# Moving the tests of a bound check to the last group but one, and a copy behind four exponentials

## The chip, the core and the metric

The kernel runs on one core of a Trainium2 chip. The metric is the device time of one launch, in microseconds (us). The core has five engines that each work through their own list of instructions in order and wait for each other through semaphores: TensorE (PE, matrix products; its weight loads are shown as PEld), VectorE (DVE), ScalarE (ACT), GpSimd (POOL) and SyncE (SP), whose list holds the DMA transfers.

## The reference

Two graph layers over 64 graphs of 256 nodes with 512 features share one adjacency matrix. Layer 0 is attention with one additive score per pair of nodes, layer 1 is attention with 8 heads of 64. All is float32.

```python
# --- layer 0 (adj_preln) ---
h = jnp.maximum(_layernorm(x, axis=-1), 0.0)
x = x + _L0_gnn_ref(h, adj, L0_gnn_W, L0_gnn_a)
# --- layer 1 (adj_preln) ---
h = jnp.maximum(_layernorm(x, axis=-1), 0.0)
x = x + _L1_gnn_ref(h, adj, L1_gnn_Wq, L1_gnn_bq, ..., L1_gnn_bo)
return x
```

Layer 1 computes `q`, `k` and `v` from `h`, `scores = q k^T / 8`, masks them by the adjacency matrix, takes the softmax over the keys, weighs `v` with it and multiplies by `Wo`. The kernel leaves out the subtraction of the row maximum in the softmax. That is allowed only where the scores are bounded, so the kernel also works out a bound from the norms of the weights. If the bound fails, a second, general version of the computation (`any_inputs`) runs after the first. The bound holds for these inputs.

## The kernel before

The 64 graphs are handled as 32 groups (`g`) of two batches (`b`). A batch's 256 nodes lie on 128 partitions in two tiles. Each group goes through three stages in a pipeline over the groups: `first_norm` and `first_layer` (the two layer norms and layer 0) two groups ahead, `project` (the products for `q`, `k`, `v`) one group ahead, and `scores`, `mask_pairs`, `weigh` and `outputs` for the group itself. The strings in `steps` say in which order pieces of these stages are issued within a batch: `S` scores, `m` mask a pair of heads, `u` a projection product, `n` a norm piece, `s` a piece of layer 0, `o` an output product. A product of two 2x2-blocked matrices is done with seven block products instead of eight, so each projection consists of seven products `pq` (or `pk`, `pv`) of four matmuls each, with sums of operands made beforehand on POOL (`sums`, from `operand_sums`).

All engine calls pass through the class `Remembers` (line 35 records them). `not_sooner` and `after` add order constraints on one engine. A scheduler then orders each engine's list within these constraints and the data's own. So an edit at one place can move an instruction of another engine.

What the change touches:

- `judge` (lines 283 to 396) is the bound check. It runs as a generator, `verdict`, in pieces among the prologue's work. Its sums of squares end in a `[128, 10]` tile `norm`. Its last piece makes five tests from `norm` in 13 small DVE instructions, which write `test`, `side`, `held` and at last `wrong`, a single integer. `run(verdict)` at line 925, before the loop over the groups, finishes whatever of it is left.
- Line 51 loads `wrong` into a register on every engine, to branch on it at the end. On SP the scheduler had put that load in the prologue, between two transfers. On the other engines it stands at the end.
- The transposition of normed rows goes by way of DRAM: DVE transposes blocks of 32 x 32 into `xt`, SP writes `xt` to DRAM (`passed`), then reads it back in four parts in another order (`moved`, line 466), and ACT copies `moved` into `hT` (`put`, line 473). `put_last` remembers the last of these copies.
- `scores` (line 749) makes eight heads' scores in four pairs, into PSUM banks `sc` that come from a ring of five (`mm`), and empties each with an exponential on ACT. The exponential's order relative to `put_last` is set at line 769, for the first group's first batch alone. At that time the last `put` is that of the second group's layer 1 (`hT1`), whose two batches are copied with two instructions each.

```python
for other in [last, *put_last] if g == b == 0 and i else [last]:
    after(made, other)
```

So the exponentials of the pairs after the first (`i` from 1) come behind the second batch's copies. The projection of the second group starts right after these scores on PE: its first two products need only the first batch's copies, and its third one needs `sums`, which POOL makes from both batches' copies, and the earlier product's bank to have been copied out by ACT (`kept_q`).

Of the kernel before, what the change touches and what calls it, by code (L numbers as in the profile page):

```python
# [57 lines left out]
def bounded(  # L58
# [35 lines left out]
    NG = B // GB  # L94
# [14 lines left out]
    def mm(name):  # L109
        return psum.tile([P, 512], F32, tag="turn", name=name, bufs=5)  # L110
# [4 lines left out]
    def after(instruction, name):  # L115

        tc.add_manual_dep(
            instruction.ins, name,
            mybir.DependencyInfo(mybir.DependencyClass.NoSync, mybir.DependencyReason.DATA),
            reason="the engine's order",  # L120
        )

    def not_sooner(engine, operation, *args, **kwargs):

        last = engine.last
        after(getattr(engine, operation)(*args, **kwargs), last)
# [9 lines left out]
    def matmul(*args, **kwargs):  # L136
        in_order(nc.tensor.matmul(*args, **kwargs))  # L137
# [116 lines left out]
    def weight_sums(name):  # L254
        w = w_sb[name]
        not_sooner(vector, "tensor_sub", w[:, :, T3, :], w[:, :, W22, :], w[:, :, W12, :])
        vector.tensor_sub(w[:, :, T1, :], w[:, :, W12, :], w[:, :, W11, :])
        vector.tensor_sub(w[:, :, T2, :], w[:, :, W22, :], w[:, :, T1, :])
        vector.tensor_sub(w[:, :, T4, :], w[:, :, W21, :], w[:, :, T2, :])
# [23 lines left out]
    def judge():  # L283
# [73 lines left out]
        norm = const.tile([P, 10], F32, name="norm")  # L357
# [3 lines left out]
        gpsimd.memset(power[:, 7:8], 1.0)  # L361
        gpsimd.memset(power[:, 8:10], 1.0 / 32)
        gpsimd.tensor_tensor(norm, norm, power, op=ALU.pow)
        for _ in range(6):
            yield
        root = float(D) ** 0.5

        test = const.tile([P, 5], F32, name="test")
# [24 lines left out]
        held = const.tile([P, 1], F32, name="held")  # L393
        vector.tensor_reduce(held, test, axis=AX.X, op=ALU.min)
        vector.tensor_scalar(wrong, held[0:1, :], -1.0, 1.0, op0=ALU.mult, op1=ALU.add)
        yield

# [9 lines left out]
    put_last, sums_last = [], []  # L409
# [334 lines left out]
    def value_differences(g, b):  # L744

        v = qkv["v", g, b][0]
        not_sooner(gpsimd, "tensor_sub", v[:, 1, :], v[:, 1, :], v[:, 0, :])

    def scores(g, b):

        (q, q_tag), (k, k_tag) = (qkv[name, g, b] for name in "qk")
        name = f"{g}_{b}"
        p = att.tile([P, NQ * QH, NT, N], F32, tag="p", name=f"p_{name}", bufs=1)
        for i in range(HP):
            sc = [mm(f"sc_{name}_{2 * i + j}").rearrange("p (k n) -> p k n", k=NT) for j in range(2)]
            for kb in range(NT):
                for j in range(2):
                    rows = slice(j * DH, (j + 1) * DH)  # L760
                    matmul(
                        sc[j][:, kb, :], k[rows, i, kb * P : (kb + 1) * P], q[rows, i, :],
                        start=True, stop=True,
                    )
            pair = p[:, 2 * i : 2 * i + 2]
            for j in range(2):
                last = scalar.last
                made = scalar.activation(pair[:, j], sc[j], AF.Exp, scale=scale)
                for other in [last, *put_last] if g == b == 0 and i else [last]:
                    after(made, other)  # L770
        places.extend((q_tag, k_tag))
        return p
# [16 lines left out]
    def weigh(g, b, p):  # L789


        v, v_tag = qkv["v", g, b]
        name = f"{g}_{b}"
        total = mm(f"total_{name}").rearrange("p (q n) -> p q n", q=NQ)
        r = att.tile([P, NQ, N], F32, tag="r", name=f"r_{name}", bufs=1)
        for quad in range(NQ):
            for j in range(QH):
                matmul(
                    total[j * S : (j + 1) * S, quad, :], ones, p[:, quad * QH + j, 0, :],
                    start=True, stop=True,  # L800
                )
        for quad in range(NQ):
            not_sooner(vector, "reciprocal", r[:, quad, :], total[:, quad, :])
        for quad in range(NQ):
            pr = mm(f"pr_{name}_{quad}").rearrange("p (h n) -> p h n", h=2)
            for half in range(2):
                for kb in range(NT):
                    for j in range(QH):
                        head = quad * QH + j
                        c0 = head * DH + half * S  # L810
                        matmul(
                            pr[j * S : (j + 1) * S, half, :], v[:, kb, c0 : c0 + S],
                            p[:, head, kb, :], start=(kb == 0), stop=(kb == NT - 1),
                        )
            oT = big.tile([P, 2, N], F32, tag=f"oT{quad}", name=f"oT_{name}_{quad}", bufs=1)
            vector.tensor_mul(oT, pr, r[:, quad, None, :].to_broadcast([P, 2, N]))
            oTs[quad] = oT
        places.append(v_tag)
        quads = [oTs[c][:, :, r * P : (r + 1) * P] for r in range(2) for c in range(2)]
        sums = big.tile([P, 3, 2, P], F32, tag="o_sums", name=f"o_sums_{g}_{b}", bufs=1)  # L820
        operand_sums(vector, quads, sums)
        operands["o", g, b] = seven(quads, sums)

    def outputs(g, b):
        xt, ops = xs[g, b], operands.pop(("o", g, b))

        def product(out, i, start):
            a, w = ops[i]
            for c in range(2):
                matmul(  # L830
                    out, a[:, c, :], w_sb["o"][:, c, w, :],
                    start=start and c == 0, stop=(c == 1), skip_group_check=True,
                )

        def add(t, half, out):
            to = xt[:, t, half * D // 2 : (half + 1) * D // 2]
            vector.tensor_add(to, out, to)

        first = held_bank(2, f"py1_{g}_{b}")[:, : D // 2]
        product(first, 1, True)  # L840
        add(0, 0, first)
        yield
        second = mm(f"py2_{g}_{b}")[:, : D // 2]
        product(second, 2, True)
        add(0, 0, second)
        yield
        product(first, 6, False)
        add(1, 0, first)
        yield
        second = mm(f"py7_{g}_{b}")[:, : D // 2]  # L850
        product(second, 7, True)
        add(1, 1, second)
        yield
        product(first, 5, False)
        add(1, 1, first)
        yield
        product(second, 4, False)
        add(1, 0, second)
        if g == NG - 1:

            nc.sync.dma_start(og[g, b][:, 1], xt[:, 1])
            nc.sync.dma_start(og[g, b][:, 0, : D // 2], xt[:, 0, : D // 2])
        yield
        product(first, 3, False)
        add(0, 1, first)
        if g == NG - 1:
            nc.sync.dma_start(og[g, b][:, 0, D // 2 :], xt[:, 0, D // 2 :])
        else:
            nc.sync.dma_start(og[g, b], xt)
        yield  # L870


    def run(part):
        for _ in part:
            pass
# [54 lines left out]
    for g in range(NG):  # L930
        products = project(g + 1) if g + 1 < NG else iter(())
        pieces = first_layer(g + 2) if g + 2 < NG else iter(())
        for b, parts in enumerate(steps):
            if g == b == 0:

                parts = "Smmnnuuuumnnmussnussuunununsu"
            if waiting is not None:
                weigh(*waiting)
                late = outputs(*waiting[:2])
            for i, part in enumerate(parts):  # L940
                if part == "u":
                    next(products, None)
                elif part == "o":
                    next(late, None)
                elif part == "s":
                    next(pieces, None)
                elif part == "n":
                    next(norms, None)
                elif part == "m":
                    next(masks)  # L950
                else:
                    waiting = (g, b, scores(g, b))
                    masks = mask_pairs(waiting[2])
                if i == (len(parts) * 3 // 4, 6)[b]:
                    value_differences(g, b)
                if i == len(parts) // 2:
                    if g == b == 0:
                        weight_sums("o")
                    if b == 0 and g + 1 < NG:
                        residual(g + 1)  # L960
                    if g + 3 < NG:
                        load(g + 3, b)
        run(products)
        run(pieces)
# [373 lines left out]
```

## Time and profile before

The median of three runs is 2489.0 us.

| What | us |
|---|---|
| runs | 2487.59, 2489.0, 2489.72 |
| the profiled execution, device time | 2488.04 |
| its span, first to last instruction | 2486.4 |
| mean granted clock of TensorE | 0.998 of full |
| DVE busy in 90 to 95 us | 4.66 of 5 |
| PE busy in 95 to 100 us | 0.69 of 5 |
| PE busy in 2404.7 to 2438 us (group 30, second batch) | 33.30 of 33.30 |
| DVE busy there | 16.69 of 33.30 |

The profile is that of one execution. A busy engine is one with an instruction in work, and what an engine waited for is inferred from semaphores. The chain of waits follows the work back from the last instruction: at each step to what released it, or to the instruction before it on its engine. Times in the views count from the span's start, while a run's time includes some 1.6 us around the span.

### The profile page before, as it was taken

To read this page: it belongs to the slowest core of one execution; us is meant where nothing else is said; L and a number is where in the kernel's file an instruction comes from. 1 tells how busy PE (TensorE), PEld (TensorE's weight loads), DVE (VectorE), ACT (ScalarE), POOL (GpSimd) and SP (SyncE) were. 2 spreads that over 40 slices of the span, in tenths; PEclk is the share of its full clock that TensorE was granted. 3 is DMA by queue.
4 is the path that set the end of the run, shared out by engine and by line. 5 is a ranking of instruction groups with operands and counts; after the bars stand their busy time and mean duration, and the time that the engine had idled before them with its cause. 6 is when DMAs were issued, how large, how long until landed. Compare 5 with 4: busy or idle time off the path is not lost.

```text
span 2486.4 us, 41322 instructions
## 1 busy us (share of the span) xinstructions
PE 2456.1 (99%) x16034; PEld 2039.9 (82%) x16034; DVE 1687.1 (68%) x3002; ACT 1011.4 (41%) x2019; POOL 1017.3 (41%) x978
## 2 busy tenths in 40 slices
PE   8899999999999999999999999999999999999998
PEld 7778888888888888888888888888888888888886
DVE  6676766776666767667766667676677666676656
ACT  5443443443443434443434434344434344344321
POOL 3533444334444334444344443344443344533332
PEclk9999999999999999999999999999999999999999
DMA  6222232322232322222222323222222223232100
GB/s 191 73 90 77 68 98 81 102 80 89 75 106 77 107 79 73 91 88 95 87 84 73 107 78 105 79 80 85 92 92 95 76 75 105 81 102 79 58 26 36
DMA packets 135129, 213.58 MB, mean 86 GB/s; under 512 B 15504, under 2 KB 80272, under 8 KB 134928
## 3 DMA queue, kind: packets, MB, share of 16 engines
q1 hardware_dynamic: 134928, 210.89, 26.0%
q8 instruction: 128, 2.10, 0.3%
q14 instruction: 73, 0.60, 0.1%
HBM read 112.20 MB, written 98.63 MB: 85 GB/s over the span
## 4 chain that ended last, share of the span: by engine, by line
PE 97%; DVE 1%; DMA 0%; ACT 0%; issue 0%; SPq 0%; ACTq 0%; DVEq 0%
PE pq L137 16%; PE pk L137 16%; PE pv L137 15%; PE py L137 15%; PE sc L137 10%; PE ph L137 9%; PE pr L137 9%; PE po L137 4%; PE total L137 3%; DVE p L35 0%; DMA w_sb<-in_L_gnn_W_dram 0%; DVE r L35 0%; PE gram_q L137 0%; PE gram_k L137 0%; DVE prod L35 0%
## 5 line engine op out<-in xcount | busy, mean ns | idle before, releaser
L35 POOL TENSOR_TENSOR p<-p 128x512 f32<-128x512 f32 x256 | 409.0, 1612 | 711.5 <-DVE p L35 711.5
L35 ACT ACTIVATE p<-sc 128x512 f32<-128x512 f32 x512 | 258.0, 627 | 237.9 <-PE sc L137 233.9
L35 DVE TENSOR_TENSOR p<-p,maskT 128x1024 f32<-128x1024 f32 x256 | 340.2, 1349 | 3.9 <-ACT p L35 3.9
L35 DVE TENSOR_TENSOR x<-py,x 128x256 f32<-128x256 f32 x448 | 185.8, 415 | 169.9 <-PE py L137 160.7
L35 ACT ACTIVATE xn<-x,factor 128x512 f32<-128x512 f32 x256 | 194.5, 807 | 209.7 <-POOL factor L35 209.7
L35 DVE RECIPROCAL r<-total 128x256 f32<-128x256 f32 x128 | 215.6, 1726 | 90.1 <-PE total L137 90.1
L137 PE MATMUL py<-wo_sb,oT 128*128 128x256 f32 x1024 | 262.5, 379 | 1.7 <-DVE x L35 1.1
L137 PE MATMUL sc<-q,k 64*128 64x256 f32 x2048 | 253.5, 389 | 8.3 <-ACT p L35 8.3
L137 PEld LDWEIGHTS sc<-q,k 64*128 64x128 f32 x2048 | 211.7, 187 | 50.3 <-issue 26.3
L137 PE MATMUL pk<-hT,wk_sb 128*128 128x256 f32 x1024 | 244.7, 382 | 0.0
L137 PE MATMUL pq<-hT,wq_sb 128*128 128x256 f32 x1024 | 242.6, 385 | 0.0
L137 PE MATMUL pv<-wv_sb,hT 128*128 128x256 f32 x1024 | 236.9, 379 | 0.0
L35 POOL TENSOR_TENSOR factor<-factor,rexp 128x2 f32<-128x2 f32 x128 | 90.5, 707 | 355.2 <-DVE factor L35 355.1
L137 PE MATMUL ph<-w_sb,hT 128*128 128x258 f32 x1024 | 234.9, 381 | 0.4 <-ACT hT L35 0.3
L137 PE MATMUL pr<-p,v 128*32 128x256 f32 x4096 | 232.7, 379 | 0.0
L137 PEld LDWEIGHTS pq<-hT,wq_sb 128*128 128x128 f32 x1024 | 193.7, 192 | 36.3 <-issue 9.9
L137 PEld LDWEIGHTS pk<-hT,wk_sb 128*128 128x128 f32 x1024 | 192.1, 190 | 35.3 <-issue 10.4
L137 PEld LDWEIGHTS ph<-w_sb,hT 128*128 128x128 f32 x1024 | 194.1, 190 | 30.4 <-ACT hT L35 0.9
L137 PEld LDWEIGHTS py<-wo_sb,oT 128*128 128x128 f32 x1024 | 194.1, 190 | 29.7 <-DVE x L35 1.5
L137 PEld LDWEIGHTS pv<-wv_sb,hT 128*128 128x128 f32 x1024 | 194.5, 190 | 26.4
L137 PEld LDWEIGHTS pr<-p,v 128*32 128x32 f32 x4096 | 133.1, 110 | 87.9
L137 PE MATMUL py<-wo_sb,o_sums 128*128 128x256 f32 x768 | 197.5, 379 | 3.6 <-DVE x L35 3.6
(124 smaller groups left out, 3640.7 us busy)
## 6 DMA issues: line engine op xcount, KB each, us to landing
passed<-xt SPq DMA_DIRECT2D x124, 512.0 KB, 2.6
moved<-passed SPq DMA_DIRECT2D x496, 128.0 KB, 3.1
x<-in_x_dram SPq DMA_DIRECT2D x64, 512.0 KB, 4.4
out_dram<-x SPq DMA_DIRECT2D x62, 512.0 KB, 3.1
own<-line SPq DMA_DIRECT2D x31, 256.0 KB, 3.1
wq_sb<-in_L_gnn_Wq_dram SPq DMA_DIRECT2D x2, 512.0 KB, 9.7
wk_sb<-in_L_gnn_Wk_dram SPq DMA_DIRECT2D x2, 512.0 KB, 10.7
wv_sb<-in_L_gnn_Wv_dram SPq DMA_DIRECT2D x2, 512.0 KB, 7.5
```

The lines of the kernel that those rows point to most:

```text
L35: instruction = getattr(self.engine, operation)(*args, **kwargs)
L137: in_order(nc.tensor.matmul(*args, **kwargs))
```

## The change

The tests leave `judge` and become a function `conclude`, which is called in the second batch of the last group but one, in the middle of its pieces. `judge` ends with `norm`. The condition on the exponentials changes from `i` to `i > 1`: the second pair's exponentials no longer have to come behind the second batch's copies.

```diff
         gpsimd.tensor_tensor(norm, norm, power, op=ALU.pow)
-        for _ in range(6):
-            yield
+        norms_found.append(norm)
+        yield
+
+    norms_found = []
+
+    def conclude():
+        (norm,) = norms_found
         root = float(D) ** 0.5
 
         test = const.tile([P, 5], F32, name="test")
@@
         held = const.tile([P, 1], F32, name="held")
         vector.tensor_reduce(held, test, axis=AX.X, op=ALU.min)
         vector.tensor_scalar(wrong, held[0:1, :], -1.0, 1.0, op0=ALU.mult, op1=ALU.add)
-        yield
@@
-                for other in [last, *put_last] if g == b == 0 and i else [last]:
+                for other in [last, *put_last] if g == b == 0 and i > 1 else [last]:
                     after(made, other)
@@
                     if g == b == 0:
                         weight_sums("o")
+                    if g == max(NG - 2, 0) and b == 1:
+                        conclude()
                     if b == 0 and g + 1 < NG:
                         residual(g + 1)
```

## The prediction

> **What bounds the kernel now.** I read the page first, for the engine that sets the end, and then the chain of work.
>
> ```profile
> PE 2456.1 (99%) x16034; PEld 2039.9 (82%) x16034; DVE 1687.1 (68%) x3002; ACT 1011.4 (41%) x2019; POOL 1017.3 (41%) x978
> PE 97%; DVE 1%; DMA 0%; ACT 0%; issue 0%; SPq 0%; ACTq 0%; DVEq 0%
> ```
>
> TensorE (PE) is busy for 2456.1 of 2486.4 us and carries 97% of the chain, and the change leaves its instruction list alone. Only an idle stretch of PE can be won or lost, some 30 us in all. So I asked for PE's waits by window (us in total, times, longest).
>
> ```profile
> PE pt L140 <- ACT xn L35: 10.2, 1, 10.2
> ...
> PE sc L137 <- ACT p L35: 6.3, 2, 5.9
> ...
> PE sc L137 <- ACT p L35: 2.0, 1, 2.0
> ```
>
> The first is the first load at the start, out of reach. The second is a gap of 0.4 and one stall of 5.9 us, in 95.69 to 101.62, in the first group's first batch. The third lies at 173.85, in the second group, where no engine's order changes. The chain in order of time (start, duration, what) crosses the 5.9 us stall like this:
>
> ```profile
> 90.03 0.69 DVE v L35
> 90.72 0.79 DVE test L35
> ...
> 94.12 0.15 DVE wrong L35
> ...
> 94.28 0.48 SPq L51
> ...
> 96.53 3.35 DMA moved<-passed
> ...
> 99.94 1.14 ACT hT L35 x2
> 101.08 0.51 ACT p L35
> ...
> 101.62 2.07 PE sc L137 x6
> 103.70 9.87 PE pq L137 x40
> 113.57 3.49 PE ph L137 x16
> ```
>
> Read backwards: PE's last score matmuls wait for a PSUM bank that the third exponential (ACT p) empties; that exponential stands on ScalarE (ACT) behind the copy `hT<-moved` of the second group's second batch (call it B); that copy waits for the `moved` transfers; those stand on SP's queue behind the load of `wrong` (L51); and that waits for the last of the bound check's tests on VectorE (DVE). SP's own waits in 80 to 110 us say what it costs:
>
> ```profile
> SPq L51 <- DVE wrong L35: 7.1, 1, 7.1
> ```
>
> The clock comes last (us, PE busy, granted clock, DMA share, GB/s):
>
> ```profile
> 98.00:99.00 1.00, 0.00 (x0) 0.97 1.04 298
> 99.00:100.00 1.00, 0.00 (x0) 0.50 0.76 306
> ...
> 104.00:105.00 1.00, 1.00 (x3) 0.50 0.71 184
> 105.00:106.00 1.00, 1.00 (x4) 0.61 0.07 19
> ```
>
> The idle stretch also halves PE's clock from 98.9 to about 105.6, so about 4 us of matmuls run at half speed: 2.0 us more.
>
> [...] B's `moved` issues at 95.21, right after the register load of 94.28, though its source was in memory when the DMA traffic ended at 90.0. [...] The trace agrees for 5.9 and for 2.0 us of idle (at 173.85, clock 0.50 in 178 to 180), but 1.74 us at 2444.2 left it at 1.00. [...] `test<-norm` took 856 ns and `side<-norm` 1132 ns while POOL's residual adds ran to 92.70; the other tests took 141 to 171 ns.
>
> **The change part by part.** The order listing of both kernels shows three differences: DVE's 13 tests move from behind the last `v` add to behind the last mask multiply of group 30's second batch; the load of `wrong` on SP moves from ahead of B's `moved` to among the last output stores; B's two copies on ACT stand behind four exponentials instead of two. Besides, SP now puts the fourth `moved` of the third group's first batch (C4) behind the `passed` of its second batch (D).
>
> *Removed tests.* 13 DVE instructions in 90.64 to 94.26, 3.6 us: the third group's statistics and transposes come that much earlier, and `passed` of its first batch goes from 97.37 to about 93.8. Nothing on PE waits for these directly.
>
> *Removed SP wait.* `passed` of B issued at 86.82 and its traffic was over by 90.0 (91.0 if it took the 4.2 us of the next `passed`, 97.37 to 101.59). B's four `moved` can then issue at 90.0 instead of 95.21, and land 4.66 us later as before (95.21 to 99.87): 94.7, at worst 95.7.
>
> *ACT's order.* Up to the second exponential nothing changes: it ends at 94.94. A queued exponential takes 2.54/5 = 0.51. Then: two more exponentials to 95.95, in which time B has landed even at its worst; B's copies, 1.04 to the next start, 97.0; four exponentials 2.03, 99.0; two `xn` 1.51, 100.5; `kept_q` 0.84, 101.4. PE: the third exponential ends at 95.45, so the last scores follow at once (seventh score's first half ended at 95.69), to 96.5; two products `pq` at 1.73 each, 99.95. The third product accumulates into the bank that `kept_q` reads, so it waits for 101.4: a new stall of 1.4 us, in place of 5.9. GpSimd's two `sums` for it take 1.26 and at most 2.13 from 97.0: 100.4, not later. In the profile the third product starts three products before `ph`: 113.57 - 3 x 1.73 = 108.38. So 108.38 - 101.4 = 7.0 us are won, the 2.0 of half clock included, provided 1.4 us of idle doesn't halve the clock. I take that it doesn't, since 1.74 us didn't[...]. A gain from it is excluded, since an idle PE does no work.
>
> *C4.* D's `passed` needs the two `xn` (100.5) and a DVE transpose of 0.7: 101.3. C4 follows at 101.65 and lands in 3.0 (the median) to 4.1: 104.7 to 105.7. Its copy on ACT comes behind the third `kept_q`, that is 101.4 + 2 x 1.73 + about 1 = 105.9. Cost nothing, hidden by those three products; without that cover it is microsecond for microsecond in front of `ph`, then some 1 us at most. D's `moved` lands at about 109 and is used at 110.4.
>
> *Tests in group 30.* They start at 2419.96 of the old trace. DVE is idle from there to 2421.93. They need about 2.0 us by the undisturbed rows (13 x 0.15), up to 3.7 with the two held ones, so the `v` add behind them, and the `x` adds behind that, come 0.1 to 1.7 late. Those free PSUM banks that PE takes again at 2426.84 (the sixth `py` product, into the bank whose add ended at 2423.1) or later: PE doesn't wait. In 2425 to 2430 DVE is busy for 1.15 of 5 us, so it has caught up by then. Without this cover it would be at most 1.7. SP's register load there waits for tests done by 2424; the store behind it issues at 2432.71. No cost.
>
> **Sum.** 7.0 us off the profiled execution's 2488.04 (span 2486.4 and 1.64 around it) is 2481.0. That execution lies 0.96 below the median of 2489.0, and before's runs spread over 2.1 us[...]; carried to the median the forecast is 2482.0.
>
> **The rivals.** *Less gain:* [...] it halves, or C4 is late by a microsecond or two: 7.0 - 1.7, or - 2: 2484. [...] against it: the tail's 1.74. *More gain:* [...] its half clock (178 to 180) goes too, 1.7: 2480.3. *B's landing is not bound by SP:* if B still came at 99.94, the reordering alone would help. PE would run on to 99.95; copies to 101.0, four exponentials to 103.0, `xn` to 104.5, `kept_q` to 105.4: 108.38 - 105.4 = 3.0 won, 2486. Against it: the 7.1 us wait, and traffic over at 90.0. This is also the case where the change doesn't do what it says. *Slower:* C4 behind D's `passed` is a new wait across engines, SP for DVE for ACT's eight exponentials. If it kept `ph` waiting from 106.6 past 113.6, the end would be later; that needs C4 to land at 113 instead of 105. With 1.7 of half clock behind it, from 111.3 on. At 114 it would be 2490 or, with the clock, 2492. The landings seen, 2.6 to 4.2 us, speak against it.
>
> **How the numbers follow.** Forecast 0.55 (2480.5 to 2483.5), more gain 0.17, less gain 0.15, B not bound by SP 0.08, slower 0.05. 0.2%, 5.0 us, is about what a measurement of this kernel can tell from no change: 2484.0 and below is faster. The forecast, more gain and a third of less gain lie there: 0.77; the rest of less gain and the 3 us case 0.18; slower 0.05. The range reaches to 2479 for more gain with a lucky median, and to 2485.5 past less gain.
>
> **What would show it.** In the changed trace: no SP wait at L51 near 90; B's `moved` issued near 90.0; the second of B's copies over by 97.1; PE's wait for ACT p gone, with a wait of about 1.4 us of `pq` for ACT `kept_q` in its place; clock 1.00 from 95 to 110; the first `ph` of the third group near 106.6, and everything behind it 7 us earlier; the stall of 2.0 us still there near 167; the tests in group 30 with PE at full there. Wrong would be: B landing after 97, a wait of `ph` for `hT` of more than 1 us, a clock of 0.50 near 103, or a PE gap near 2415.

## The result and the profile after

The changed kernel takes 2481.43 us (median of 9 runs, 2480.54 to 2483.24), the kernel before 2489.14 (9 runs, 2487.59 to 2489.74). The ratio is 0.997, with a 95% interval of 0.9959 to 0.998: faster, by 7.7 us of medians, a small gain but clear of the scatter. The letters B, C4 and D name transfers as in the prediction. The profiled execution took 2481.28 us with a span of 2479.5, against 2488.04 and 2486.4: 6.9 us.

The page of the changed kernel, its line of busy times and the chain's shares by engine:

```profile
PE 2454.1 (99%) x16034; PEld 2040.6 (82%) x16034; DVE 1690.7 (68%) x3002; ACT 1011.0 (41%) x2019; POOL 1017.6 (41%) x978
PE 97%; DVE 1%; DMA 1%; ACT 0%; issue 0%; POOL 0%; SPq 0%; ACTq 0%; DVEq 0%
```

PE is still the bound, with the same 16034 matmuls. Its busy time fell by 2.0 us from 2456.1, which is the half clock (98.9 to 105.6 before) that no longer follows the first stall. PE's waits of the changed kernel in 100 to 2400 us (us in total, times, longest):

```profile
PE sc L137 <- ACT p L35: 2.0, 1, 2.0
PE pq L137 <- POOL hT L35: 0.9, 1, 0.9
```

The 5.9 us of waiting for an exponential are gone, and a wait of 0.9 us of a `pq` product has come in. The 2.0 us stall of the second group is still there. SP's waits of the changed kernel in 80 to 110 us:

```profile
SPq L35 <- DVE xt L35: 20.3, 3, 15.9
SPq L470 <- DMA passed<-xt: 9.7, 4, 3.2
SPq L470 <- ACT hT L35: 0.3, 1, 0.3
```

L51 is not among them, so no transfer here waits for the tests any more. What is left is a wait for a transfer's own data or buffer, or for the transfer ahead of it in SP's order. The chain of the changed kernel over the place where the stall was (start, duration, what):

```profile
86.93 3.58 DMA passed<-xt
...
91.87 2.66 DMA moved<-passed
94.54 1.47 ACT p L35 x3
96.01 1.03 ACT hT L35 x2
...
97.11 1.46 POOL sums L35
...
98.63 1.27 POOL sums L35
99.91 1.24 POOL hT L35
...
101.27 5.42 PE pq L137 x24
106.68 3.49 PE ph L137 x16
```

B's `moved` land at 94.5 instead of 99.9. The first `ph` of the third group starts at 106.68 where it started at 113.57: 6.89 us earlier. That is the whole difference of the spans, so gains and losses elsewhere in the 2480 us come to nothing together. The clock in the new stall (us, PE busy, granted clock, DMA share, GB/s):

```profile
100.00:101.00 1.00, 0.35 (x2) 0.00 (x0) 1.00 (x2) 1.00 (x3) 1.00 (x1) 1.00 0.00 0
101.00:102.00 1.00, 0.73 (x4) 0.69 (x5) 0.98 (x3) 0.12 (x1) 1.00 (x2) 1.00 0.00 0
```

The field behind POOL's is the clock: 1.00, although PE idles for 0.9 us here. And the tests at their new place, DVE's and POOL's timelines of the changed kernel in group 30 (start, duration, engine, operation, idle before):

```profile
2412.99 0.15 DVE L35 TENSOR_TENSOR test<-norm 128x1 f32<-128x1 f32 x1
...
2413.21 1.27 POOL L35 TENSOR_TENSOR p<-p 128x512 f32<-128x512 f32 x1 [1.32 <-DVE test L35]
2413.24 1.26 DVE L35 TENSOR_SCALAR side<-norm 128x2 f32<-128x2 f32 x1
...
2415.89 0.14 DVE L35 TENSOR_SCALAR wrong<-held 1x1 int32<-1x1 f32 x1
2415.97 0.69 DVE L35 TENSOR_TENSOR v<-pv,kept_v 128x512 f32<-128x512 f32 x1
```

The 13 tests take 3.0 us, of which `side<-norm` took 1.26 us beside an operation of POOL. The `v` add follows on them at once, and PE has no wait there: of its waits between 100 and 2400 us the two above are all, and behind 2400 us they are those of the kernel before.

### The profile page after: what moved, and what is told of

Same layout as the page of the kernel before. It is cut to its first block, busy times and chain, and to the rows that moved or that the text cites. A ratio compares the mean times of both kernels' runs of the same rounds, so it can differ in the third digit from the quotient of the medians.

```text
span 2479.5 us, 41322 instructions
## 1 busy us (share of the span) xinstructions
PE 2454.1 (99%) x16034; PEld 2040.6 (82%) x16034; DVE 1690.7 (68%) x3002; ACT 1011.0 (41%) x2019; POOL 1017.6 (41%) x978
## 4 chain that ended last, share of the span: by engine, by line
PE 97%; DVE 1%; DMA 1%; ACT 0%; issue 0%; POOL 0%; SPq 0%; ACTq 0%; DVEq 0%
PE pq L137 16%; PE pk L137 16%; PE py L137 15%; PE pv L137 15%; PE sc L137 10%; PE ph L137 9%; PE pr L137 9%; PE po L137 4%; PE total L137 3%; DVE p L35 0%; DMA w_sb<-in_L_gnn_W_dram 0%; DVE r L35 0%; PE gram_q L137 0%; DMA passed<-xt 0%; PE gram_k L137 0%
```

## The experiments

The theory of the prediction: the gain is SP's wait for `wrong`, which held B's `moved` back, plus the half clock that followed the stall (98.9 to 105.6); the new order of the exponentials is needed to turn B's earlier landing into an earlier product. The rivals: the order alone does it; the 3.6 us of DVE work do it; or the moved tests cost something at the other end. The first four kernels ran beside a kernel before of 2488.38 us (31 runs), the last three beside one of 2488.4 (11 runs).

The profiled executions don't reach the first group's scores at the same moment: they begin on PE at 91.65 before and 91.75 in the changed kernel, but at 91.21 with the tests moved alone, 92.14 with the order alone, 92.11 with SP's wait alone and 92.58 with the early `kept_q`. Where times of two traces are compared below, this offset is part of the difference.

### The move of the tests alone

```diff
-                for other in [last, *put_last] if g == b == 0 and i > 1 else [last]:
+                for other in [last, *put_last] if g == b == 0 and i else [last]:
```

> The tests and SP's load stand in group 30 as in the changed kernel; the exponentials keep the old order (B's copies behind two). Theory (ScalarE's total work up to kept_q decides, and SP's wait was the cause): B's copies start at about 95, the seventh and eighth scores wait about 0.9 us for the third exponential, kept_q still ends at 101.1, so the third projection product of the second group still starts at 101.3 and the whole gain stays: 2481.5, ratio 0.997. Rival (both parts are needed, the copies in front of the third exponential hold PE as before): 2485 or more.

Measured: 2481.89 us (8 runs), ratio 0.9975 (0.9964 to 0.9985). The gain is there without the new order. The chain of this kernel shows how:

```profile
94.55 1.14 ACT hT L35 x2
95.69 0.50 ACT p L35
...
96.23 1.13 PE sc L137 x6
97.36 8.95 PE pq L137 x40
106.31 3.49 PE ph L137 x16
```

Once B lands in time, the third exponential stands only 1.14 us behind the copies, and the scores wait for it at 96.23 for 1.0 us. Then all five products run without a gap: PE comes to the third one at 100.89, a microsecond of waiting later than it would have, and `kept_q` ended at 100.75. So with the old order the small stall lies in the scores, with the new order (0.9 us) in front of the third product. The edit of the exponentials is worth nothing that these runs can measure once the tests are gone from the prologue.

### The new order alone

```diff
-                for other in [last, *put_last] if g == b == 0 and i else [last]:
+                for other in [last, *put_last] if g == b == 0 and i > 1 else [last]:
```

This is the kernel before with the other part of the change.

> The exponentials' new order, with the tests and SP's load of wrong in the prologue as before. Theory: B's moved still issues at 95.2 and lands at 99.9; PE runs on to about 100 with two projection products and then waits 5.4 us for kept_q, to 105.4, and since that idle stretch is as long as the old one the clock halves behind it: 3.0 us won, about 2.0 given back, 2488, ratio 0.9995. Rival (the order on ScalarE is what won the time): 2482. Without the clock's part: 2486.

Measured: 2487.1 us (13 runs, 2485.91 to 2491.17), ratio 0.9998 (0.9989 to 1.0006), which isn't told from no change; as 11 of the 13 runs lie below the median of the kernel before, a gain of about a microsecond isn't excluded. PE's waits of this kernel, and two windows of it:

```profile
PE pq L137 <- ACT kept_q L35: 5.2, 1, 5.2
```

```profile
104.00:105.00 1.00, 0.00 (x0) 0.00 (x0) 0.64 (x1) 1.00 (x3) 1.00 (x2) 0.50 0.67 213
107.00:108.00 1.00, 1.00 (x4) 0.82 (x3) 1.00 (x2) 0.00 (x0) 1.00 (x1) 0.50 1.02 336
```

The stall only changes its place: the scores run through, and the third product waits instead, because `kept_q` stands on ACT behind B's copies, which begin at 100.54. That product starts at 105.91, which is 108.38 - 105.91 = 2.5 us early, or 3.0 without the offset of 0.5, and the half clock falls on it and its two followers: they take 113.75 - 105.91 = 7.84 us instead of 3 x 1.73 = 5.2, 2.7 us more. So the first `ph` comes at 113.75, as late as before (113.57). That profiled span, 2484.3, is nevertheless 2.1 us below that of before. The stall of the second group wasn't followed by a half clock in it, which is 1.7 of the 2.1.

### SP's wait alone

```diff
+        early = const.tile([1, 1], I32, name="early")
-        vector.tensor_scalar(wrong, held[0:1, :], -1.0, 1.0, op0=ALU.mult, op1=ALU.add)
+        vector.tensor_scalar(early, held[0:1, :], -1.0, 1.0, op0=ALU.mult, op1=ALU.add)
+        found.append(early)
@@
+    found = []
@@
+                    if g == max(NG - 2, 0) and b == 1:
+                        not_sooner(vector, "tensor_copy", wrong, found[0])
```

This is the kernel before with these lines and with the new order of the exponentials. The tests stay in the prologue, and only a copy of one integer is made in group 30.

> All 13 tests stay on VectorE in the prologue and write a tile of their own; a copy of one element in group 30 writes wrong, so that SP's load stands late. The exponentials have the new order. Theory (SP's wait costs, the 3.6 us of VectorE do not): 2481.5, third product at 101.3, ratio 0.997. Rival (VectorE's time is part of it): the third group's statistics come 3.6 us late, and 1 to 4 us of the gain are missing, 2483 to 2486.

Measured: 2482.84 us (14 runs), ratio 0.9978 (0.997 to 0.9986). PE's waits of this kernel:

```profile
PE ph L137 <- ACT hT L35: 1.5, 2, 1.2
PE pq L137 <- ACT kept_q L35: 0.9, 1, 0.9
```

Its chain in front of that `ph`:

```profile
96.59 1.21 DVE xt L35 x2
97.80 2.72 DVE p L35 x2
...
102.02 1.30 DVE xt L35 x2
...
103.34 0.34 SPq L35
...
103.74 3.70 DMA moved<-passed
...
107.53 0.63 ACT hT L35
...
108.20 3.75 PE ph L137 x16
```

So 5.5 us (2488.38 - 2482.84) of the gain are SP's wait. The rest hangs on the DVE time. With the tests at 91.09 to 94.71, the third group's first transposes come at 96.5 instead of 92.81 and the two mask multiplies behind them only end when D's normed rows have been ready for over a microsecond (since 100.74). D's transposes start at 102.02 instead of 99.72, D's `passed` issues at 103.34 instead of 101.16, and C4, which stands right behind it on SP, lands 107.4. The `ph` waits for C4's copy: 1.2 us. (Of each of these differences 0.36 us is the offset.) So each of the two expectations was right in part: most of the gain is SP's wait, and a part of about a microsecond is the DVE time. By time alone this kernel isn't told apart from the whole change, as the two intervals overlap; the wait is what shows it.

### The earlier copy ahead of the norm

```diff
-                parts = "Smmnnuuuumnnmussnussuunununsu"
+                parts = "Smmunnuuumnnmussnussuunununsu"
```

This one tests who holds the third product in the changed kernel. The trace names POOL (`hT`, 99.91 to 101.15), while by the program it should be ACT's `kept_q`, which ends at 101.12. One product piece is issued ahead of the two norm pieces, so that `kept_q` comes ahead of the two `xn`.

> The changed kernel, with the first kept_q of the second group ahead of the third group's second pair of xn on ScalarE. Theory (the new 0.9 us stall of the third product is a wait for kept_q, as the prediction had it): kept_q ends near 99.8, the third product follows the second at about 100.4, 0.9 us won, 2480.6. Rival (it is a wait for GpSimd's third sum, which the trace names, over at 101.13): the third product still starts at 101.3 and nothing is won, 2481.5.

Measured: 2480.64 us (7 runs), ratio 0.997 (0.9959 to 0.9982). ACT's timeline of this kernel:

```profile
99.67 0.90 ACT L35 ACTIVATE kept_q<-pq,bq_sb 128x256 f32<-128x256 f32 x2
```

PE's:

```profile
101.03 1.89 PE L137 MATMUL pq<-sums,wq_sb 128*128 128x256 f32 x8
112.19 2.01 PE L137 MATMUL ph<-w_sb,hT 128*128 128x258 f32 x8 [0.61 <-ACT hT L35]
```

and POOL's:

```profile
100.70 1.28 POOL L35 TENSOR_TENSOR hT<-hT 128x512 f32<-128x512 f32 x1
```

The third product follows on the second with no wait, while POOL's operation runs on to 101.98. So it was `kept_q` that held it. The 0.9 us are won there, and 0.6 of them are lost again: D's `passed` issues at 104.36 instead of 101.16 (0.8 of it is the offset), and the second `ph` waits for D at 112.19. The `xn` are later now, and on DVE the `q` add and a mask multiply (101.30 to 103.12) stand ahead of D's transposes, where the changed kernel has them behind. No gain can be measured. The profiled execution is one of the longer ones of this kernel (2483.19); the section on the hardware says what it met.

### The same cure for the second stall

```diff
-    put_last, sums_last = [], []
+    put_last, sums_last, norm_last = [], [], []
@@
+            norm_last[:] = [scalar.last]
@@
-                for other in [last, *put_last] if g == b == 0 and i > 1 else [last]:
+                others = [last, *put_last] if g == b == 0 and i > 1 else [last]
+                if g == 1 and b == 0:
+                    others = [last, *put_last, *norm_last]
+                for other in others:
```

The stall of 2.0 us near 167 has the form of the first one: ACT's timeline of the changed kernel there.

```profile
164.91 1.08 ACT L35 ACTIVATE p<-sc 128x512 f32<-128x512 f32 x2 [5.85 <-PE sc L137]
165.88 1.14 ACT L35 COPY hT<-moved 128x512 f32<-128x512 f32 x2
166.90 1.53 ACT L35 ACTIVATE xn<-x,factor 128x512 f32<-128x512 f32 x2
168.33 3.02 ACT L35 ACTIVATE p<-sc 128x512 f32<-128x512 f32 x6
```

The scores' banks wait behind two copies and two `xn`, though ACT had been idle for 5.85 us before the first exponential. In this kernel the copies and the `xn` stand ahead of all eight exponentials of that batch, in the idle time.

> The changed kernel, with all exponentials of the second group's first batch behind the third group's copies and the xn before them on ScalarE (in the third group and later the order is so already). Theory (the 2.0 us stall near 167 is the same kind of thing, copies and xn between two exponentials, and it carries a half-clock window): the stall and its window go, 2.0 to 3.7 us won, 2478 to 2479.5. Rival (the copies or xn are themselves late there, and now hold all exponentials): the stall stays or grows, 2481.5 or more.

Measured: 2476.73 us (5 runs, 2476.0 to 2478.8), ratio 0.9955 (0.9942 to 0.9969). This beats both kernels, and by more than the expected 2478 to 2479.5. ACT's timeline of it:

```profile
159.35 1.14 ACT L35 COPY hT<-moved 128x512 f32<-128x512 f32 x2
160.39 1.52 ACT L35 ACTIVATE xn<-x,factor 128x512 f32<-128x512 f32 x2
165.25 4.03 ACT L35 ACTIVATE p<-sc 128x512 f32<-128x512 f32 x8 [3.33 <-PE sc L137]
```

Copies and `xn` are over before the scores begin on PE at 164.08; the 32 score matmuls then run through. The clock is 1.00 all through 160 to 182. Set against the changed kernel, the second group's last `ph` starts at 185.34 instead of 189.12: 3.8 us, which is the 2.0 of the stall and about 1.7 of the half clock that had followed it (half of 3.4 us at 0.50, in 170.5 to 173.9). The spans differ by 4.6 (2479.5 - 2474.9). The last `x` add on DVE, with which the chain ends, still starts 3.8 us earlier (2469.86 against 2473.66), so the other 0.8 lies behind it, in the end of the program with its last store; what it is stays open.

### Both together

The two edits above in one kernel, with nothing else changed.

> kept_first and second_stall together: the two gains add, 0.9 and 2.0 to 3.7, 2477 to 2478.5. If the half-clock window of the one hides the other's gain, 2479.

Measured: 2478.51 us (5 runs), ratio 0.9958 (0.9944 to 0.9971), not told apart from the kernel with the second stall's cure alone. PE waits 0.8 us for the second `ph`'s copy here. Set against the second stall's cure alone, this kernel starts its scores 0.5 us later (92.39 against 91.91) and the second group's first `pk` product behind its last `ph` 0.1 us later (189.80 against 189.69), so about 0.4 us of the earlier `kept_q` is left and the rest is taken back at D. That this profile is nevertheless 1.9 us longer is for the most part a half clock near its end (0.50 in 2456 to 2459), which the other doesn't have.

### The tests thirty times

```diff
-                    if g == max(NG - 2, 0) and b == 1:
+                    if 1 <= g <= max(NG - 2, 0) and b == 1:
```

The tests run in the groups 1 to 30, with their tiles made once. If they cost anything at their new place, it shows thirtyfold.

> The changed kernel, with the 13 tests repeated in the second batch of each of the groups 1 to 30, in 30 places instead of one; the answer is the same. Theory (VectorE has idle time there, and PSUM banks come free in time): under 0.1 us each, 2481.5 to 2484. Rival (the cover is thin, and a late v or x add holds PE): 0.7 to 1.7 us each, 2500 to 2530.

Measured: 2481.08 us (7 runs), ratio 0.9972 (0.9961 to 0.9983): the time of the changed kernel. The traces are sharper than the medians. From the second group's first `pk` product behind its last `ph` to the column sums (`total`) behind group 30's last batch PE takes 2250.90 us in both kernels (192.24 to 2443.14 here, 193.47 to 2444.37 in the changed kernel), with all thirty places in between. So the tests cost nothing at their new place. PE's waits of it behind 100 us, those of the changed kernel:

```profile
PE sc L137 <- ACT p L35: 2.4, 2, 2.0
PE pq L137 <- POOL hT L35: 0.9, 1, 0.9
```

Not tried: the old order of the exponentials together with the second stall's cure.

Runs of one kernel scatter by 2 to 5 us, even with the cure and its second stall gone (2476.0 to 2478.8). Much of that goes with the clock: of the tests moved alone, the four runs with a mean granted clock of 0.999 take 2480.2 to 2480.71 and the four with 0.998 take 2483.06 to 2484.25. The traces show two places where a half clock comes or doesn't come. One is the second stall, the other the end. PE near the end of the thirty tests and of the changed kernel (us, PE busy, granted clock, DMA share, GB/s), a line of each:

```profile
2459.00:2460.00 1.00, 1.00 (x3) 0.50 0.00 0
2460.00:2461.00 1.00, 1.00 (x5) 1.00 0.00 0
```

The thirty tests gain 1.7 us on the changed kernel behind the second stall and lose 1.7 here, so the two equal times are made up differently.

## Why the prediction was right

The forecast was 7.0 us on the profiled execution; 6.8 us of its time (2488.04 to 2481.28) and 6.9 of its span went. By steps:

- **The binding wait.** Right, by the chain read backwards: SP's register load held B's `moved`. With the load gone they issued at 90.58 (90.0 forecast) and landed at 94.5 (94.7). The kernel that took away SP's wait and kept the tests had 5.5 of the 7.7 us.
- **The steps on ACT.** Right to 0.3 us: B's copies 95.88 to 97.03 (95.95 to 97.0), `kept_q` over at 101.12 (101.4), the third product at 101.27 (101.4).
- **The new stall.** Foreseen with its cause, but set at 1.4 where it measured 0.91 us. PE's two products ended at 100.35, not at 99.95: they began 0.13 later than forecast (96.63), and the timeline gives the two 3.72 where the forecast counted 2 x 1.73 = 3.46. This changed only the length of the idle time, not the end: the third product's start was taken from ACT. The trace named POOL for this wait, yet the run with an early `kept_q` showed that the forecast's cause is the true one.
- **The half clock.** Right: the stretch from 98.9 to 105.6 runs at 1.00 now. The new order alone, with 5.2 us of stall, had it back (0.50 in 104.0 to 110.8). The 1.7 us that the forecast sets for a half clock is an estimate, half of the 3.41 us at 0.50 behind the second stall before (177.4 to 180.8). The reason given for the 1.4 us, that 1.74 us near the end had left the clock at 1.00, was one case and partly luck: in the profiles of the thirty tests and of both orders two waits of 1.3 and 1.1 us near the end were followed by a half clock.
- **The second stall.** The forecast left it as it was, and both profiles have a half clock behind it that takes 1.7 us (half of 3.41 us at 0.50). That is luck: other executions have none or twice as much, and the difference of two profiles could have come out at 5 or at 9 us with the same cause.
- **The tests on DVE.** "Nothing on PE waits for these directly" holds, but the removal isn't worthless, as that sentence let it seem: through the masks and D's `passed` it decides when C4 comes, and with the tests left in place `ph` waited 1.2 us. The forecast time was right because it counted C4's landing with the tests gone (104.7 to 105.7; its copy began at 105.72).
- **The order of the exponentials.** The forecast took the whole change as one sum and did not say what the order adds. It adds nothing measurable: without it the scores wait 1.0 us where the product would wait 0.9.
- **The tests in group 30.** No cost, as forecast; 3.0 us, inside its 2.0 to 3.7. The thirtyfold run bears the "nothing" out.
- **The rival "B's landing is not bound by SP".** It was priced at 3.0 us won, and the run that had this situation won almost nothing at that place: 3.0 us by the order, as priced (2.5 with the offset), and 2.7 back by the half clock, which that case had left out.
- **The two held tests.** The prediction sets both beside POOL's adds. `side<-norm` ended with POOL's operation in both kernels (92.73 and 92.70 before, 2414.50 and 2414.48 after), but `test<-test` took 0.15 us under the same POOL operation (91.53). Why the two took longer is not shown. The forecast takes from them their measured times alone.

On the chip's side, what carried the case is a wait on SP that held the transfers behind it in SP's order. Before, SP waited 7.1 us for `wrong`, its register load came at 94.28, and B's `moved` issued at 95.21. In the kernel with SP's wait alone removed, the same transfers issue at 90.86, although the tests still stand on DVE, from 91.09 to 94.71.

## What to carry to other kernels

A register load between the transfers of SP was a wait for the transfers behind it here (7.1 us, four `moved`): look for such a load in the own waits of a queue that issues DMAs, and put the value's last write late, where its queue has nothing urgent. When a stall ends on an engine with a fixed order, read what stands between the releaser and the instruction that is waited for; moving those instructions into idle time ahead (as in the second group, 4 us by the medians, each set against its own kernel before) is worth more than shifting which of two consumers waits (0.9 won, 0.6 given back). Where a stall has a half clock behind it (2.0 and 1.7 us in the second group), price both, also in the rival cases.

## What the runs showed of the hardware

A stall of 2.0 us of PE was followed by half clock in some executions and not in others, with the same instructions around it. In the profiles of before, of the change, of the tests moved alone and of SP's wait alone about 3.4 us at 0.50 came after it; in that of the early `kept_q` 6.8 us; in those of the order alone and of the thirty tests none. The window of the changed kernel, the clock again the third field from the end:

```profile
171.00:172.00 1.00, 1.00 (x4) 0.77 (x3) 0.16 (x1) 0.35 (x1) 1.00 (x1) 0.50 1.10 259
```

and the same window of the thirty tests, some 2 us after the same stall:

```profile
171.00:172.00 1.00, 1.00 (x6) 0.87 (x5) 0.62 (x1) 0.81 (x2) 1.00 (x1) 1.00 1.00 304
```

Four matmuls in a microsecond against six. So the price of such a stall is 2.0 us, 3.7 or, with two stretches of half clock, 5.4 (an estimate: 2.0 and half of the time at 0.50), and one profile doesn't tell which.

The clock record of the traces gives the moments. In the profiles of before and of the change each half clock begins a whole number of times 3.413 us after the record's first entry, which is full clock (from 13.61 us on before): 25, 48 and 724 times before, 46 and 722 in the changed kernel. Those in the midst of the program last 6.83 and 3.41 us before and 3.41 in the changed kernel; by the windows they last 3.4 with the tests moved alone and with SP's wait alone, and 6.8 with the order alone and with the early `kept_q`. What decides whether a half clock follows a stall is not shown, nor how much idle time it takes. With the tests moved alone 1.6 us of the stall lay in the 3.4 us before the half clock; before, the 1.74 us near the end (2444.2 to 2445.94) were followed by 1.00.
